# Gathering edge rows straight from `dst` and `src`: the padded copies go, and GpSimd masks the rows that were shifted back

## The chip, the cores and the metric

The kernel runs on one core of one Trainium2 chip. Its engines are named as in the profile: PE (TensorE), PEld (the weight loads of TensorE), DVE (VectorE), ACT (ScalarE), POOL (GpSimd) and SP (SyncE, which here only starts DMAs). The metric is the device time of one execution in microseconds. The kernel before took 1608.21 us, the median of three runs (1603.38 to 1609.29).

## The reference, cut to what matters

A graph has 6250 nodes with 64 features and 200,000 edges, and the edges are sorted by `dst`. Two GraphSAGE layers, then three message-passing layers with batch norm, each sum something over the edges into each node:

```python
def sage_conv(x, src, dst, W_l, b_l, W_r, n_nodes):
    msg = x[src]
    agg = jax.ops.segment_sum(msg, dst, num_segments=n_nodes)
    ...
    return mean @ W_l.T + b_l + x @ W_r.T

def _mp_layer(x, src_f, dst_f, ea_f, W, b):
    m = jnp.concatenate([x[dst_f], x[src_f], ea_f], axis=1) @ W.T + b
    agg = jax.ops.segment_sum(m, dst_f, num_segments=n)
    return jax.nn.relu(agg)
```

All five layers use the same edges. The kernel therefore builds the matrix of edge counts once (which node sends how many edges to which), and each layer is then a matrix product with it.

## The kernel before, in words

**Stages.** The first third of the execution is the build: it turns the two integer lists into 13 column tiles of the count matrix, 512 destination nodes wide, in 8-bit floats. As tiles become ready, the first SAGE layer is applied to them (`first_layer`, L724), and each tile is stored to DRAM (`adj8`, L1029). After the build come the second SAGE layer together with the edge attributes (up to 900 us or so) and the three message layers, which read the tiles back. The change touches only the build.

**Slots and columns.** The work of the build is cut into 2569 slots. A slot is a run of 128 consecutive edges together with a window of at most 10 destination nodes; 128 slots make a column t, and there are 21 columns, t = 0 to 20. `SEARCH` names five groups of columns. For each group the kernel looks up where each slot's first edge lies: `near_samples` (L824) compares samples of `dst`, `gather_behind` (L840) fetches 400 numbers behind the sample for each slot by an indirect DMA on GpSimd's queue (L843), and `first_edges` (L847) counts in them (L852) and writes the positions into `start_i` (L860, L864).

**Rows, keys, one-hots.** `fetch(t)` (L891) brings in the 128 `dst` and the 128 `src` numbers of each of the column's slots, one row of 128 numbers per partition, by two indirect DMAs on GpSimd's queue (L896) whose offsets are read from `start_i`. `columns(t)` (L900) makes two keys of them on DVE: L905 (`hi`), L906 (key 0, from the rows and `hi`), L907 (key 1), and L908, which subtracts the window's first key and clips to 2000, so that edges outside the window match nothing. PE transposes both keys (L913), ACT copies them to 16 bits, each number twice (`k2`, L915). From `k2` DVE makes one-hots (`one_hots`, L628): `lo` tiles of 16 slots, one-hot in the source, and `rhs` tiles of up to 2048 columns, one-hot in the destination. PE multiplies them slot by slot into PSUM (`pair`, L1012) and ACT moves full windows into the tile `a` (L1019, L1024).

**Padded copies.** A slot that begins fewer than 128 edges before the end of the list would read past it. So both lists are first copied into DRAM tensors `ends` (L543) that are longer by PADE (L519 to L521). Two buffers are filled on GpSimd, with 8191 for `dst` and 0 for `src` (L792, L793), and stored behind the copies (L797); 8191 is a node that no window holds. The copies themselves are two DMAs from DRAM to DRAM (L802). Column 0 does not wait for them: it reads the inputs (L894), with its starts clipped to E - 128 (L859), and the edges that the shift brings in front of the slot's own are masked by the tensor `passed` (L861, L862, L910). All later columns read `ends`.

**What sets the order.** Each engine works through its own list in order. `on_slot` (L919) fixes where the work of the next columns is called for: at slot 0 of column t `fetch(t+1)` and, at the columns that `SEARCH` names, `first_edges` or `near_samples` and `gather_behind`; at slot 64 `columns(t+1)`. `pin` keeps an instruction in the order of the program against other pinned ones; the rest a scheduler may move. Buffers set how far one engine runs ahead of another: `rows` and `key` have two (`ework`, L764), `lo` and `rhs` three each (`hot`, L765), `hi` one.

In the compiled order of before, GpSimd's list for the columns is only indirect DMAs: `fetch(t+2)` is free to go as soon as column t's keys no longer need the `rows` buffer. The transposes L913 of column t stand in PE's list at slot 96 for t = 1, 171 for t = 2, 320, 456, 577, 715, 848, 968 and so on, between none and 85 slots ahead of column t's first slot.

Of the kernel before, what the change touches and what calls it, by code (L numbers as in the profile page):

```python
# [13 lines left out]
BF16 = mybir.dt.bfloat16  # L14
F8 = mybir.dt.float8e3
I32 = mybir.dt.int32
AF = mybir.ActivationFunctionType
ALU = mybir.AluOpType
# [4 lines left out]
P = 128  # L23
# [385 lines left out]

NONE = 8191
NSMP = 4


# [2 lines left out]
EAG = 32  # L418
# [56 lines left out]
def gnn_kernel(ctx: ExitStack, tc: tile.TileContext, x, src, dst, ea, W_l1, b_l1, W_r1, W_l2, b_l2, W_r2,  # L475
# [26 lines left out]
    wins = window_plan(N, E)  # L502
# [7 lines left out]
    R = -(-NS // P)  # L510
    subs = []
    for b in range(NB):
        n, c = slots_for(expected(N, E, b * P, (b + 1) * P)), 0
# [2 lines left out]
            c += EAG  # L516
    assert len(subs) <= P
    last_b = {b: i for i, (b, _, _) in enumerate(subs)}
    PADE = P * (max(max(k for _, _, k in ws) for ws in wins) + 1)  # L519
    PADE = max(PADE, P * EAG)  # L520
    PADE = -(-PADE // 64) * 64  # L521


    c_np = np.zeros((P, 3, R + 1), np.float32)
# [15 lines left out]
    t_dram = nc.inline_tensor(t_np, name="first_edges")  # L540

    dram = ctx.enter_context(tc.tile_pool(name="fdram", bufs=1, space=DRAM))
    ends = [dram.tile([E + PADE, 1], I32, name=f"ends{i}") for i in range(2)]  # L543
    adj8 = [dram.tile([P, NB * tw(j)], mybir.dt.uint8, name=f"adj8_{j}") for j in range(NT)]
    ok_t = None

    with ExitStack() as fast:
# [203 lines left out]
        with ExitStack() as bld:  # L751
            ep = bld.enter_context(tc.tile_pool(name="edge", bufs=1))
            tab = ep.tile([P, 3, R + 1], F32, name="tab")
            etab = ep.tile([P, 3, NSUB], F32, name="etab")
            start_i = ep.tile([P, R + 1], I32, name="start_i")
# [3 lines left out]
            iota = ep.tile([P, 512], F16, name="iota")  # L759
# [4 lines left out]
            ew = slots.enter_context(tc.tile_pool(name="ework", bufs=2))  # L764
# [19 lines left out]
            thr = room[:EP, 4 * NPAD - 2 * P * (R + 1):].bitcast(mybir.dt.int16)  # L784
            early = SEARCH[1][1] * P
            t_ap = t_dram.ap() if hasattr(t_dram, "ap") else t_dram
            pad = spare(2 * PADE // 64).bitcast(I32).rearrange("p (i c) -> p i c", i=2)

            nc.sync.dma_start(smp, dst.rearrange("(p q c) -> p q c", p=EP, q=NSMP)[:, :, 0])
            nc.scalar.dma_start(thr[:, :early], t_ap[:, :early].to_broadcast([EP, early]))  # L790
            nc.scalar.dma_start(tab, c_dram.ap() if hasattr(c_dram, "ap") else c_dram)
            nc.gpsimd.memset(pad[:, 0, :], NONE)  # L792
            nc.gpsimd.memset(pad[:, 1, :], 0)  # L793
            one = pp.tile([P, 1], BF16, name="one")
            nc.gpsimd.memset(one, 1.0)
            for end, i in zip(ends, range(2)):
                pin(nc.scalar.dma_start(end[E:, :].rearrange("(p c) o -> p (c o)", p=64), pad[:64, i, :]))  # L797
            low = parts[1].rearrange("p b c -> p (b c)").bitcast(F32)
            early_weights = load_weights(low)
            for end, of, eng in ((ends[0], dst, nc.sync), (ends[1], src, nc.scalar)):  # L800

                pin(eng.dma_start(end[0: E, :].rearrange("(c p k) o -> p c (k o)", p=16, k=500),  # L802
                                  of.rearrange("(c p k) -> p c k", p=16, k=500)))
            nc.gpsimd.memset(parts[0][:, :, 3 * D: 3 * D + 1], 1.0)
            smf = pp.tile([EP, NSMP], F32, name="smf")
            nc.vector.tensor_copy(smf, smp)
# [40 lines left out]
            def first_edges(g):  # L847

                t0, t1 = SEARCH[g][0], min(SEARCH[g][1], R + 1)
                s = slice(t0, t1)  # L850
                for t in range(t0, t1):
                    pin(nc.vector.tensor_scalar(junk, blks[t % most], tab[:, 0, t: t + 1], None,  # L852
                                                ALU.is_lt, ALU.add, accum_out=c2[:, t: t + 1]))
                nc.vector.scalar_tensor_tensor(near[:, s], near[:, s], float(GAP), c2[:, s], ALU.mult, ALU.add)
                nc.vector.tensor_add(near[:, s], near[:, s], tab[:, 1, s])
                if g == 0:


                    nc.vector.tensor_single_scalar(near[:, R: R + 1], near[:, s], float(E - P), ALU.min)  # L859
                    nc.vector.tensor_copy(start_i[:, s], near[:, R: R + 1])  # L860
                    nc.vector.tensor_sub(near[:, s], near[:, s], near[:, R: R + 1])  # L861
                    nc.vector.tensor_scalar(passed, iota[:, :P], near[:, s], 4000.0, ALU.is_lt, ALU.mult)  # L862
                else:
                    pin(nc.vector.tensor_copy(start_i[:, s], near[:, s]))  # L864

            def first_attributes():

# [23 lines left out]
            def fetch(t):  # L891

                fetched[t] = rows = ew.tile([P, 2, P], I32, name="rows")
                of = [v.rearrange("(e o) -> e o", o=1) for v in (dst, src)] if t == 0 else [end[:, :] for end in ends]  # L894
                for end, i in zip(of, range(2)):
                    pin(nc.gpsimd.indirect_dma_start(  # L896
                        out=rows[:, i, :], out_offset=None, in_=end,
                        in_offset=bass.IndirectOffsetOnAxis(ap=start_i[:, t: t + 1], axis=0)))

            def columns(t):  # L900
# [4 lines left out]
                pin(nc.vector.tensor_single_scalar(hi, rows[:, 1, :], 7, ALU.logical_shift_right))  # L905
                nc.vector.scalar_tensor_tensor(key[:, 0, :], rows[:, 0, :], float(NB), hi, ALU.mult, ALU.add)  # L906
                nc.vector.scalar_tensor_tensor(key[:, 1, :], hi, -float(P), rows[:, 1, :], ALU.mult, ALU.add)  # L907
                nc.vector.tensor_scalar(key[:, 0, :], key[:, 0, :], tab[:, 2, t: t + 1], 2000.0, ALU.subtract, ALU.min)  # L908
                if t == 0:
                    nc.vector.tensor_add(key[:, 0, :], key[:, 0, :], passed)  # L910
                kp = psm.tile([P, 2, P], F32, name="lin")
# [380 lines left out]
```

## Time and profile before

| | before |
|---|---|
| median of three runs | 1608.21 us |
| the profiled execution, whole | 1605.75 us |
| its span, first to last instruction | 1604.0 us |
| granted TensorE clock | 0.977 |
| PE busy, share of the span | 1488.1 us, 93% |
| DVE busy | 905.4 us, 56% |
| ACT busy | 575.4 us, 36% |
| POOL busy, instructions | 217.7 us, 93 instructions |
| the copies to `ends` | 2 DMAs of 781.2 KB |
| `fetch` from `ends` | 40 indirect DMAs, median 3.5 us from issue to landing |
| `gather_behind` | 22 indirect DMAs, median 3.6 us from issue to landing |

The whole time is 1.75 us longer than the span. Busy shares are means over stages with different limits. Over the build (to about 540 us) DVE is busy nearly without a break for the first 200 us; over the rest of the execution PE is. In answers of the trace a row of the timeline is: start and duration in us, engine, line, operation, output and input tile, sizes, count, and in brackets the idle time before it and what ended it.

### The profile page before, as it was taken

Reading aid. Unit: us, or ns where it says so; the run is one execution under the profiler, and the core shown is the slowest. Engines: PE = TensorE matmul, PEld = TensorE weight load, DVE = VectorE, ACT = ScalarE, POOL = GpSimd, SP = SyncE. Lnnn points to the kernel's source line nnn. Section 1 sums busy time; section 2 is a strip of 40 time slices with the busy share of each in tenths; the row PEclk is TensorE's granted clock in tenths of the full one; section 3 lists DMA queues with packets and bytes.
Section 4 is the critical chain, followed back from the end, with each engine's and each line's share of the span. In section 5 each row is a group of like instructions: output and inputs, shape, how many; then the busy total and the mean of one; then the engine's idle time right before and its main releaser. Section 6 shows DMA issues by size and latency. Waiting matters only on the chain.

```text
span 1604.0 us, 38502 instructions
## 1 busy us (share of the span) xinstructions
PE 1488.1 (93%) x17115; PEld 1370.7 (85%) x17115; DVE 905.4 (56%) x1499; ACT 575.4 (36%) x1086; POOL 217.7 (14%) x93
## 2 busy tenths in 40 slices
PE   3887799999998999999999999999899999999997
PEld 2666688888886898899899989889799999899997
DVE  5899998988968509987986511111431112442222
ACT  2737476777848404544553200000310000310000
POOL 2465830731601100000000000000000000000000
PEclk9898999999999999999999999999899999899998
DMA  5302232320421536435344354443345444164540
GB/s 135 125 29 96 46 100 88 154 99 4 169 85 71 226 160 243 174 131 200 135 146 148 135 241 161 162 171 122 132 167 220 177 175 168 81 247 173 197 163 11
DMA packets 45200, 227.32 MB, mean 142 GB/s; under 512 B 23621, under 2 KB 31650, under 8 KB 37343
## 3 DMA queue, kind: packets, MB, share of 16 engines
q1 hardware_dynamic: 37965, 139.40, 23.1%
q10 hardware_dynamic: 4306, 78.10, 12.4%
q0 software_dynamic: 2752, 7.26, 1.6%
q8 instruction: 136, 2.23, 0.5%
q14 instruction: 41, 0.34, 0.1%
HBM read 183.77 MB, written 42.57 MB: 141 GB/s over the span
## 4 chain that ended last, share of the span: by engine, by line
PE 65%; DVE 17%; issue 7%; ACT 6%; DMA 3%; POOL 2%; ACTq 0%; DVEq 0%; POOLq 0%
PE agg L666 49%; PE pair L1012 7%; DVE lo L628 6%; ACT a L1019 3%; DVE rhs L628 2%; PE u L1166 2%; POOL parts L843 2%; DVE e L1070 2%; PE bank L1079 1%; DVE z L693 1%; DMA e<-in_edge_attr_dram 1%; DVE e L1072 1%; PE lin L1188 1%; PE tr L718 1%; PE lin L740 1%
## 5 line engine op out<-in xcount | busy, mean ns | idle before, releaser
L666 PE MATMUL agg<-parts,a 128*128 128x192 bf16 (+1 forms) x12005 | 1088.2, 247 | 4.4 <-DVE parts L649 1.3
L666 PEld LDWEIGHTS <-a 128*128 128x128 fp8e3 x12005 | 1006.4, 98 | 30.5 <-issue 19.6
L1019 ACT ACTIVATE a<-pair 128x784 fp8e3<-128x784 f32 (+3 forms) x355 | 294.2, 900 | 106.2 <-PE pair L1012 90.4
L1012 PE MATMUL pair<-rhs,lo 128*128 128x147 bf16 (+5 forms) x2569 | 259.4, 237 | 43.7 <-ACT a L1019 17.0
L1012 PEld LDWEIGHTS <-lo 128*128 128x128 bf16 x2569 | 191.6, 100 | 97.6 <-issue 49.2
L628 DVE TENSOR_TENSOR rhs<-iota,k 128x1960 bf16<-128x1960 f16 (+15 forms) x240 | 239.5, 1020 | 18.5 <-ACT k L915 10.5
L628 DVE TENSOR_TENSOR lo<-iota,k 128x2048 bf16<-128x2048 f16 x161 | 195.7, 1220 | 1.9 <-ACT k L915 1.3
L693 DVE TENSOR_REDUCE z<-agg 128x256 f32<-128x768 f32 (+1 forms) x39 | 35.3, 910 | 271.8 <-PE agg L666 271.4
L896 POOL DMA_INDIRECT rows<-ends,start_i x40 | 140.4, 3510 | 180.3 <-DVE key L908 154.1
L628 DVE TENSOR_TENSOR lo<-iota,e_d 128x2048 bf16<-128x2048 f16 (+11 forms) x132 | 130.9, 1012 | 19.6 <-PE bank L1079 17.6
L1079 PE MATMUL bank<-lo,lhs 128*128 128x128 bf16 x1701 | 107.6, 219 | 17.6 <-ACT lhs L1073 12.4
L1079 PEld LDWEIGHTS <-lhs 128*128 128x128 bf16 x1701 | 98.3, 98 | 29.1 <-ACT lhs L1073 20.4
L693 DVE TENSOR_REDUCE nd<-agg 128x256 f32<-128x768 f32 (+1 forms) x26 | 23.5, 907 | 116.5 <-PE agg L666 110.8
L1182 POOL TENSOR_TENSOR nd<-res,inv 128x256 f32<-128x256 f32 (+1 forms) x13 | 7.6, 588 | 550.2 <-DVE z L1128 341.2
L720 ACT COPY mx<-tr 128x512 f32<-128x512 f32 (+1 forms) x26 | 14.7, 566 | 169.7 <-PE tr L718 169.6
L709 ACT ACTIVATE sp_r<-z 128x256 f32<-128x256 f32 (+1 forms) x26 | 10.5, 403 | 172.2 <-DVE z L708 172.0
L1206 ACT ACTIVATE hr<-hr 64x512 f32<-64x512 f32 (+1 forms) x13 | 7.9, 605 | 172.2 <-DVE hr L1205 172.2
L843 POOL DMA_INDIRECT parts<-in_dst_dram,pos x22 | 53.9, 2448 | 41.0 <-DVE pos L838 31.6
L1069 ACT CAST lhs<-e 128x512 bf16<-128x512 f32 (+21 forms) x72 | 36.1, 503 | 64.0 <-PE bank L1079 43.4
L1070 DVE TENSOR_TENSOR e<-e,lhs 128x512 f32<-128x512 f32 (+21 forms) x72 | 39.5, 552 | 14.9 <-ACT lhs L1069 14.7
L1191 DVE TENSOR_SCALAR ext<-lin 64x512 f32<-64x512 f32 (+1 forms) x13 | 8.6, 663 | 68.5 <-ACT hr L1189 68.5
L1073 ACT CAST lhs<-e 128x512 bf16<-128x512 f32 (+21 forms) x72 | 36.4, 505 | 23.1 <-DVE e L1072 22.6
(149 smaller groups left out, 816.4 us busy)
## 6 DMA issues: line engine op xcount, KB each, us to landing
a<-adj SPq DMA_DIRECT2D x24, 3136.0 KB
a<-adj ACTq DMA_DIRECT2D x24, 3136.0 KB
adj<-a SPq DMA_DIRECT2D x12, 3136.0 KB
e<-in_edge_attr_dram SPq DMA_DIRECT2D x25, 256.0 KB
a<-adj SPq DMA_DIRECT2D x4, 784.0 KB
out_dram<-z SPq DMA_DIRECT2D x12, 128.0 KB
e<-in_edge_attr_dram SPq DMA_DIRECT2D x7, 152.0 KB
adj<-a SPq DMA_DIRECT2D x1, 784.0 KB
```

Of the source, the lines that this page charges most:

```text
L628: nc.vector.tensor_tensor(to.rearrange("p g (h two) -> p g h two", two=2), iota[:, :n].rearrange("p (h two) -> p h two", two=2).unsqueeze( ...
L666: nc.tensor.matmul(sums[k][:, i, :n], views[k][:, b, i * P: (i + 1) * P], pt[:, b, :n], start=(b == sources[0] and terms is None and not ( ...
L693: nc.vector.tensor_reduce(to, ps[:, :nb, : 3 * D].rearrange("p b (r d) -> p b d r", r=3), AX.X, ALU.add)
L843: pin(nc.gpsimd.indirect_dma_start(out=blks[t % most], out_offset=None, in_=dst.rearrange("(e o) -> e o", o=1), in_offset=bass.IndirectOff ...
L896: pin(nc.gpsimd.indirect_dma_start(out=rows[:, i, :], out_offset=None, in_=end, in_offset=bass.IndirectOffsetOnAxis(ap=start_i[:, t: t + 1 ...
L1012: nc.tensor.matmul(pair[:, bank % 2, col: col + wc], lo_hot(t, c), rhs[:, i, :wc], start=first, stop=last)
L1019: nc.scalar.activation(av[:, :, o: o + 2 * nd].rearrange("p h (two d) -> p h two d", two=2), pair[:, :, : nd * NB].rearrange("p two (d h) ...
L1069: nc.scalar.copy(lhs[:, :g, 0:EC], r)
L1070: nc.vector.tensor_sub(r, r, lhs[:, :g, 0:EC])
L1073: nc.scalar.copy(lhs[:, :g, 2 * EC:3 * EC], r)
L1079: nc.tensor.matmul(ps[:, :P], lhs[:, q, :], oh[:, q % HOT, :], start=(c == 0 and q == 0), stop=(i == last_b[b] and q == g - 1))
L1166: pin(nc.tensor.matmul(u[:, i, :], y[:, i * P: (i + 1) * P], maps[n - 1], start=True, stop=True))
```

## The change

- `ends`, its padding, the two fills on GpSimd, the two padding stores and the two copies are gone.
- `first_edges` clips every group's starts to E - 128 (into `c2`), writes `start_i` from the clipped value, and keeps in `c2` by how many edges each slot was shifted. This is one clip and one subtraction more on DVE for each of groups 1 to 4; group 0 had them.
- `fetch(t)` reads `dst` and `src` themselves for every t.
- In `columns(t)` for t above 0 three instructions run on GpSimd: `none` (1 where the place in the row is before the shift, times 8188 x 49), an addition of `none` to key 0, and the subtraction and clipping of key 0, which was L908 on DVE. For t = 0 the latter stays on DVE.

The changed kernel has 58 more instructions on GpSimd's list, 60 for the columns less two fills. In the compiled order GpSimd's list for a column is now: the addition and the clipping of column t, the two DMAs of `fetch(t+1)`, `none` of column t+1, then the addition and clipping of column t+1. The gathers of L843 stand between `none` and the addition of column 2 (six), of column 4 (five, behind the fill of L1038) and of column 6 (six). On PE the transposes of the keys stand at slot 101 for t = 1 and within 8 slots of where they were for all others. Off the build nothing differs.

```diff
-NONE = 8191
+NONE = 8188.0
...
-    ends = [dram.tile([E + PADE, 1], I32, name=f"ends{i}") for i in range(2)]
...
-            nc.gpsimd.memset(pad[:, 0, :], NONE)
-            nc.gpsimd.memset(pad[:, 1, :], 0)
...
-            for end, i in zip(ends, range(2)):
-                pin(nc.scalar.dma_start(end[E:, :].rearrange("(p c) o -> p (c o)", p=64), pad[:64, i, :]))
...
-            for end, of, eng in ((ends[0], dst, nc.sync), (ends[1], src, nc.scalar)):
-                pin(eng.dma_start(end[0: E, :].rearrange("(c p k) o -> p c (k o)", p=16, k=500),
-                                  of.rearrange("(c p k) -> p c k", p=16, k=500)))
...
+                nc.vector.tensor_single_scalar(c2[:, s], near[:, s], float(E - P), ALU.min)
+                pin(nc.vector.tensor_copy(start_i[:, s], c2[:, s]))
+                nc.vector.tensor_sub(c2[:, s], near[:, s], c2[:, s])
                 if g == 0:
-                    nc.vector.tensor_single_scalar(near[:, R: R + 1], near[:, s], float(E - P), ALU.min)
-                    nc.vector.tensor_copy(start_i[:, s], near[:, R: R + 1])
-                    nc.vector.tensor_sub(near[:, s], near[:, s], near[:, R: R + 1])
-                    nc.vector.tensor_scalar(passed, iota[:, :P], near[:, s], 4000.0, ALU.is_lt, ALU.mult)
-                else:
-                    pin(nc.vector.tensor_copy(start_i[:, s], near[:, s]))
+                    nc.vector.tensor_scalar(passed, iota[:, :P], c2[:, s], 4000.0, ALU.is_lt, ALU.mult)
...
-                of = [v.rearrange("(e o) -> e o", o=1) for v in (dst, src)] if t == 0 else [end[:, :] for end in ends]
-                for end, i in zip(of, range(2)):
+                for v, i in zip((dst, src), range(2)):
                     pin(nc.gpsimd.indirect_dma_start(
-                        out=rows[:, i, :], out_offset=None, in_=end,
+                        out=rows[:, i, :], out_offset=None, in_=v.rearrange("(e o) -> e o", o=1),
                         in_offset=bass.IndirectOffsetOnAxis(ap=start_i[:, t: t + 1], axis=0)))
...
-                nc.vector.tensor_scalar(key[:, 0, :], key[:, 0, :], tab[:, 2, t: t + 1], 2000.0, ALU.subtract, ALU.min)
+                if t:
+                    none = ew.tile([P, P], BF16, name="none", bufs=1)
+                    nc.gpsimd.tensor_scalar(none, iota[:, :P], c2[:, t: t + 1], NONE * NB, ALU.is_lt, ALU.mult)
+                    nc.gpsimd.tensor_tensor(key[:, 0, :], key[:, 0, :], none, ALU.add)
+                (nc.gpsimd if t else nc.vector).tensor_scalar(key[:, 0, :], key[:, 0, :], tab[:, 2, t: t + 1], 2000.0, ALU.subtract, ALU.min)
```

More of the change, by code (lines that the diff above doesn't have):

```diff
@@ L518, in gnn_kernel @@
     last_b = {b: i for i, (b, _, _) in enumerate(subs)}
-    PADE = P * (max(max(k for _, _, k in ws) for ws in wins) + 1)
-    PADE = max(PADE, P * EAG)
-    PADE = -(-PADE // 64) * 64
     c_np = np.zeros((P, 3, R + 1), np.float32)
@@ L786, in gnn_kernel @@
             t_ap = t_dram.ap() if hasattr(t_dram, "ap") else t_dram
-            pad = spare(2 * PADE // 64).bitcast(I32).rearrange("p (i c) -> p i c", i=2)
             nc.sync.dma_start(smp, dst.rearrange("(p q c) -> p q c", p=EP, q=NSMP)[:, :, 0])
```

## The prediction

> **What bounds the kernel now.** I read the busy time by stage first, because the change touches only the build. Columns: stretch, its length, then busy time (and count) of PE, PEld, DVE, ACT, POOL, the clock, DMA share and GB/s.
>
> ```profile
> 129.00:152.00 23.00, 16.91 (x159) 13.79 (x159) 23.00 (x32) 16.44 (x21) 10.08 (x1) 0.78 0.17 71
> 235.00:266.00 31.00, 29.83 (x321) 26.60 (x320) 25.49 (x35) 14.61 (x25) 3.78 (x2) 1.00 0.33 116
> 291.00:313.00 22.00, 21.76 (x261) 20.45 (x259) 22.00 (x23) 14.31 (x19) 21.74 (x1) 1.00 0.31 130
> 1250.00:1604.00 354.00, 338.00 (x3884) 331.42 (x3881) 93.07 (x224) 32.35 (x77) 0.00 (x0) 0.97 0.40 156
> ```
>
> Early in the build DVE is busy for all of 23 us and PE for 16.91: DVE sets the pace. From about 210 us PE does, with DVE close behind, in places both. After 540 us it is PE alone. POOL's 21.74 us in the third row are one single instruction, and that is the row that this change turns on. So second the timelines of POOL and DVE there.
>
> ```profile
> 235.25 1.88 POOL L896 DMA_INDIRECT rows<-ends,start_i  x1 [14.25 <-DVE key L908]
> ...
> 291.26 22.88 POOL L896 DMA_INDIRECT rows<-ends,start_i  x1 [20.93 <-DVE key L908]
> 314.45 1.98 POOL L896 DMA_INDIRECT rows<-ends,start_i  x1 [0.30 <-issue]
> ```
> ```profile
> 310.47 1.18 DVE L628 TENSOR_TENSOR rhs<-iota,k 128x1960 bf16<-128x1960 f16 x1
> 311.56 0.23 DVE L905 TENSOR_SCALAR hi<-rows 128x128 int32<-128x128 int32 x1
> 311.69 1.23 DVE L628 TENSOR_TENSOR lo<-iota,k 128x2048 bf16<-128x2048 f16 x1
> 312.83 0.30 DVE L906 SCALAR_TENSOR_TENSOR key<-rows,hi 128x128 f32<-128x128 int32 x1
> 313.03 0.30 DVE L907 SCALAR_TENSOR_TENSOR key<-hi,rows 128x128 f32<-128x128 int32 x1
> 313.23 0.29 DVE L908 TENSOR_SCALAR key<-key,tab 128x128 f32<-128x128 f32 x1
> 313.43 0.17 DVE L729 COPY cnt<-agg 128x4 f32<-128x4 f32 x1
> ```
>
> A gather whose shortest time is 0.94 us took 22.88 us. It ended at 314.14, and 0.94 us before that is 313.20: the start of L908. From 291.10 to there DVE ran one-hots (L628) and L905 to L907 without a break. The same subtraction puts the 9.20 us gather of 95.23 at 103.49 (L908 at 103.51), the 10.95 us one of 141.92 at 151.93 (L908 at 151.96), the 15.22 us one of 401.91 at 416.19 (L908 at 416.23), and the 7.76 us one of 104.73 at 111.55 (the copy L729 at 111.58). So while DVE works without a break on operations with two inputs in SBUF, an instruction of POOL that reads SBUF doesn't get in; it gets in when DVE has a gap or does something with one input, and L908 is such an opening once per column. Where DVE itself is held back by PE (235 us), POOL got in at the next end of a DVE instruction, 1.88 us.
>
> Third, how closely PE follows the keys, and the start of the build.
>
> ```profile
> 129.08 0.28 DVE L908 TENSOR_SCALAR key<-key,tab 128x128 f32<-128x128 f32 x1
> ...
> 129.42 0.44 PE L913 MATMUL lin<-ident,key 128*128 128x128 f32 x2
> ```
> ```profile
> 6.67 1.26 POOL L843 DMA_INDIRECT parts<-in_dst_dram,pos  x1 [3.89 <-DVE ext L830]
> ...
> 14.04 0.63 DVE L852 TENSOR_SCALAR_CACHE_REDUCE parts<-parts,tab 128x400 bf16<-128x400 int32 x1 [5.65 <-DMA parts<-in_dst_dram,pos]
> ```
>
> PE takes up the transposes 0.3 to 1.1 us after the start of L908 for t = 1 to 5, 7 to 9, 12, 16 and 20: it is there and waits, or nearly. For t = 6 it comes 2.6 us after, and only for t = 10, 11, 13 to 15 and 17 to 19 by 4 to 15 us.
>
> **The change, part by part.**
>
> *Copies and padding gone.* The first gather took 7.4 us from issue to use; the median of its kind is 3.6. The two copies (781.2 KB each, read and written) run just then. Nothing of the build can start before it, so their removal is worth 7.4 - 3.6 = 3.8 us at most, and nothing if the first gather is slow for another reason. I take 3.7. POOL's fills (0.14 us each) lay idle time away; `fetch` of later columns never waited for the copies.
>
> *DVE.* L908 goes: 20 times the 0.2 us between its start and its successor's, 4 us, of which the 2 us of the columns where DVE sets the pace count. Against it come 8 operations on at most 6 columns, 0.16 us long and 0.07 apart by L854 and L855: 0.5 us. The clip and copy put `start_i` one one-hot (1.2 us) later for t = 1; DVE's list takes the rows up one one-hot later too, so that is nothing.
>
> *The key on POOL.* No row shows an elementwise operation of POOL beside DVE's one-hots. Alone: the addition is half of L1182 (588 ns for 256 columns), 0.3 us; the clip and `none` like L552 on POOL, 0.54 us each. Beside one-hots I bound the wait from both sides. Below: no wait, 0.84 us for addition and clip against 0.28 of L908. Above: the gather's row, until DVE has an opening. The Trainium skill (SBUF — State Buffer, "Who interferes with whom") speaks against the change, but mildly: a DVE instruction with two SBUF inputs and a GpSimd instruction that reads SBUF exclude each other, and the later blocks until the other *instruction* has finished. By that rule each of three instructions waits at most one one-hot, 1.2 us, and the keys come 0.3 + 0.54 + 2 x 1.2 = 3.2 us after L907. By the row the wait lasts 16 to 22 us, over 10 to 19 instructions. The measurement decides: I take the row's wait where DVE sets the pace, and the rule's where PE does, as at 235 us. L908, the opening that freed the gathers, is itself removed from DVE.
>
> What ends the wait is then DVE's own want of work. PE stands at L913 and frees no `lo` or `rhs`; DVE fills the two or so free buffers of each (up to 4 x 1.15 = 4.6 us) and stops; POOL gets in. Behind PE's wait are queued its `pair` products and the first layer's; for them wait ACT and, for buffers and `k2`, DVE. DVE's loss per **stop**: addition, clip and two hand-overs of 0.3 us, 1.4; transposes 0.44 and a hand-over 0.1; some 8 to 16 products until a buffer is free, 1.1. Together 3.0 us. PE waits longer (4.6 + 1.4 = 6), but works off its store afterwards faster than DVE makes new.
>
> Column by column, by what stands ahead on POOL's list:
> - t = 1, 3, 5, 7, 9, 12, 16, 20: a stop each, 8 x 3.0 = 24.
> - t = 2: six gathers end at 68.2 us as before, DVE is near PE's pace there: 1.5.
> - t = 4: `none`, the fill (2.0) and five gathers (1.25 apart) stand ahead of the addition, and DVE has no opening between 93.6 and 111.6: 3.0 + 0.5 + 2.3 + 6.2 = 12.
> - t = 6: `none` and six gathers, 8 us, and a stop, 3; DVE has 3.7 us of L852 to do as they land and idled 1.9 there before: 6.
> - t = 8, 13, 17: `fetch(t)` now comes after the clip of t-1, one column later than before, and no opening lies between: DVE waits for rows, 0.94 and 1.5 of landing, 2.4 each, 7; t = 8 has a stop besides, 3.
> - the other columns: PE comes late enough, POOL gets in at the next end of an instruction: 0.
>
> Sum 53.5. About 4 of it fall on gaps that DVE had anyway (2.0 us between 54 and 57, for one). `none` is covered by the 20 us of a column; without that cover it would add 0.5 + a wait to each.
>
> Total: 53.5 - 4 - 3.7 - 2 + 0.5 = +44. From the profiled execution, 1605.75 + 44 = 1650; the median of the runs lies 2.5 above it: **1652 us**.
>
> **The rivals.**
> - *POOL takes its turn* (the rule holds everywhere). Keys 3.2 us late; PE has a column's 8 to 85 slots in hand, but DVE is blocked while POOL holds the port: 1.4 us in 11 columns, 15 us, less 5.2 of gains: +10, **1618 us**. For it: 235.25, 68.50 and 70.11 us, where POOL got in at an instruction's end. Against it: five waits of 9 to 23 us.
> - *Hidden, and faster* (the other side). Elementwise instructions get in at once in the 0.2 us hand-overs, or DVE's stops fall on its own slack; then 3.7 of the start and 4 of L908 remain: **1600 us**. It decides for this if POOL's two instructions end within 0.3 us or so of where L908 ended, or PE comes later than they do. For it: PE's lists allow 40 slots on average before DVE needs `k2`. Against: PE stands at L913 first.
> - *Starved throughout.* Each fetch, too, waits until DVE runs dry, in all 20 columns: 20 x (3.0 + 2.4) = 108, less 15 for DVE's slack after 210 us: **1690 to 1700 us**. For it: five instructions per column now need an opening, before two. Against: L693, L729 and L852 open several per column.
>
> **How the numbers follow.** Stops 0.62, turn-taking 0.18, hidden 0.10, starved 0.10. A measurement of this kernel can tell about 0.5% (8 us) from no change, that is 1600 to 1616. Faster: half of hidden, 0.05. Same: the other half and half of turn-taking, 0.14. Slower: the rest, 0.81. The stops' own range is 1625 to 1680 (stops of 2 to 5 us); to the turn-taking case below and part of the starved one above: 1604 to 1690.
>
> **What would show it.** Right: POOL's L895 and L896 of the changed kernel with means of many us, ending when DVE goes idle; PE waiting at its transposes for POOL's key, 3 to 8 us in each early column; DVE idle in the build up by 45 us, most before 210 us; the first L852 near 10.3 us; nothing changed behind the build but the shift. Wrong: POOL's instructions of 0.3 to 1.5 us, and PE's wait for keys as short as before. The total would be off if POOL's addition gets the port in the middle of a run of one-hots, or if late PE makes up more than I let it.

## The result, and the profile after

The changed kernel takes **1659.42 us** (median of 4 runs, 1657.8 to 1662.12) against 1605.8 us for the kernel before (4 runs, 1602.68 to 1609.29): 1.0339 times, with a 95% interval of 1.0314 to 1.0364. Its profiled execution took 1657.85 us, with a span of 1656.0 us and a granted clock of 0.959 (before: 1604.0 and 0.977). The end of the build can be read from POOL's filling of `lhs`, the first thing behind it: 588.53 us against 540.08. So 48.5 of the 52.0 us of span are lost in the build; the other 3.5 us come up again at the end of this account.

The first view is again the busy time by stage, now of the changed kernel, over the same work as the four rows of before: column 5, column 10, column 12, and the last 354 us. Columns as before.

```profile
137.90:168.10 30.20, 19.76 (x181) 16.79 (x180) 23.01 (x31) 17.16 (x21) 17.96 (x11) 0.66 0.21 78
262.80:294.20 31.40, 30.02 (x322) 26.67 (x321) 25.72 (x34) 14.10 (x24) 9.64 (x5) 1.00 0.29 110
319.60:347.70 28.10, 22.33 (x246) 21.40 (x244) 22.00 (x24) 13.17 (x17) 9.29 (x5) 0.88 0.29 120
1302.00:1656.00 354.00, 336.51 (x3881) 329.76 (x3878) 92.93 (x224) 32.29 (x77) 0.00 (x0) 0.98 0.41 156
```

DVE does the same 22 to 23 us of work in columns 5 and 12, but now stands for 7.2 and 6.1 us in them. Column 10, where PE sets the pace, and the last stage are as they were. Note the clock, the third figure from the end: 1.00 in column 12 before, 0.88 now. In column 5 it was 0.78 before already, and is 0.66.

What happens in column 5 is in three timelines of the changed kernel: first POOL, then DVE, then PE.

```profile
137.89 5.82 POOL L895 TENSOR_TENSOR key<-key,none 128x128 f32<-128x128 f32 x1 [17.25 <-DVE key L890]
143.81 0.72 POOL L896 TENSOR_SCALAR key<-key,tab 128x128 f32<-128x128 f32 x1
```
```profile
142.20 1.23 DVE L624 TENSOR_TENSOR lo<-iota,k 128x2048 bf16<-128x2048 f16 x1
147.57 1.16 DVE L624 TENSOR_TENSOR rhs<-iota,k 128x1924 bf16<-128x1924 f16 x1 [4.14 <-PE pair L1000]
```
```profile
137.80 0.42 PE L1000 MATMUL pair<-rhs,lo 128*128 128x147 bf16 x4 [0.28 <-ACT a L1007]
144.59 0.69 PE L901 MATMUL lin<-ident,key 128*128 128x128 f32 x2 [6.37 <-POOL key L896]
145.07 1.19 PE L1000 MATMUL pair<-rhs,lo 128*128 128x147 bf16 x8
```

POOL's addition (L895) takes 0.44 us where it is alone. Here it began at 137.89, the moment the keys were there, and ended at 143.71. Take 0.44 off and it really got going at 143.27; DVE's last one-hot ended at 143.43. Within 0.2 us, it was let in when DVE ran dry. PE stood 6.37 us for the key, and DVE then 4.14 us for PE. This is the stop of the prediction.

Over the whole build, these two groups of the changed kernel's page carry it (busy time, mean ns of one; idle time ahead and what ended it):

```profile
L895 POOL TENSOR_TENSOR key<-key,none 128x128 f32<-128x128 f32 x20 | 57.7, 2887 | 270.8 <-DVE key L890 211.6
...
L901 PE MATMUL lin<-ident,key 128*128 128x128 f32 x42 | 11.7, 367 | 60.9 <-POOL key L896 51.8
```

To see which columns stopped, I took the time from one column's `hi` to the next in both traces and subtracted. Eight columns grew by 4.5 us or more: 2 (4.6), 3 (6.7), 5 (7.2), 8 (4.5), 9 (7.6), 12 (6.1), 16 (5.1) and 20 (6.9), together 48.7 us. The other twelve grew by 3.7 us in all. The start is 3.9 us earlier. 48.7 + 3.7 - 3.9 = 48.5.

Column 2 is not like the other seven. Its addition was not shut out by one-hots; it stood on POOL's list behind six gathers (the last begins at 64.21 us) and then took the 0.44 us that it takes alone:

```profile
65.42 0.44 POOL L895 TENSOR_TENSOR key<-key,none 128x128 f32<-128x128 f32 x1
```

In three kernels below PE does not wait for POOL at all. There column 2 still grows by 4.2, 0.4 and 6.3 us, while column 1 shrinks by 3.9, 1.1 and 2.7 us. How much of its 4.6 us is POOL's is therefore not settled.

The start, in DVE's timeline of the changed kernel: the first count was at 14.04 us before.

```profile
10.16 0.63 DVE L839 TENSOR_SCALAR_CACHE_REDUCE parts<-parts,tab 128x400 bf16<-128x400 int32 x1 [1.67 <-DMA parts<-in_dst_dram,pos]
```

And one thing the prediction did not have: the clock around the stop of column 12, in the changed kernel's busy time by stretch.

```profile
320.50:323.00 2.50, 0.76 (x8) 0.38 (x5) 2.50 (x3) 0.91 (x2) 2.50 (x1) 1.00 1.13 482
323.00:326.90 3.90, 0.00 (x0) 0.00 (x0) 2.76 (x3) 0.00 (x0) 3.76 (x2) 0.78 0.96 412
326.90:328.50 1.60, 1.58 (x9) 1.45 (x10) 0.00 (x0) 0.58 (x1) 1.06 (x2) 0.50 0.01 0
328.50:330.50 2.00, 2.00 (x15) 1.83 (x14) 0.09 (x1) 0.83 (x1) 1.66 (x2) 0.50 0.25 66
330.50:333.00 2.50, 2.50 (x23) 2.40 (x21) 1.09 (x1) 0.83 (x1) 0.00 (x0) 0.70 0.00 0
```

PE is idle for 5.59 us (to 326.92). When it restarts, the granted clock is 0.50, and it stays below 1.00 for about 5 us, just when DVE waits for the products.

### The profile page after: what moved, and what is told of

It reads as the page before. It is cut to its first block, busy times and chain, and to the rows that moved or that the text cites. A ratio compares the mean times of both kernels' runs of the same rounds, so it can differ in the third digit from the quotient of the medians.

```text
span 1656.0 us, 38564 instructions
## 1 busy us (share of the span) xinstructions
PE 1500.3 (91%) x17115; PEld 1387.3 (84%) x17115; DVE 906.9 (55%) x1487; ACT 575.9 (35%) x1086; POOL 208.5 (13%) x151
## 4 chain that ended last, share of the span: by engine, by line
PE 48%; DVE 10%; DMA 3%; ACT 2%; issue 2%; POOL 0%; SPq 0%; ACTq 0%; DVEq 0%; POOLq 0%
PE agg L662 41%; DVE lo L624 4%; DMA e<-in_edge_attr_dram 2%; PE u L1154 2%; DMA a<-adj 2%; PE bank L1067 1%; DVE e L1058 1%; DVE z L689 1%; DVE e L1060 1%; PE lin L1176 1%; PE lin L1175 1%; PE pair L1000 1%; PE agg L669 0%; PE tr L714 0%; ACT lhs L1061 0%
## 5 line engine op out<-in xcount | busy, mean ns | idle before, releaser
L1000 PE MATMUL pair<-rhs,lo 128*128 128x147 bf16 (+5 forms) x2569 | 269.0, 244 | 34.1 <-ACT a L1007 15.2
L1000 PEld LDWEIGHTS <-lo 128*128 128x128 bf16 x2569 | 203.2, 104 | 81.2 <-issue 42.7
L1067 PE MATMUL bank<-lo,lhs 128*128 128x128 bf16 x1701 | 107.5, 219 | 17.9 <-ACT lhs L1061 12.1
L895 POOL TENSOR_TENSOR key<-key,none 128x128 f32<-128x128 f32 x20 | 57.7, 2887 | 270.8 <-DVE key L890 211.6
L901 PE MATMUL lin<-ident,key 128*128 128x128 f32 x42 | 11.7, 367 | 60.9 <-POOL key L896 51.8
L901 PEld LDWEIGHTS lin<-ident,key 128*128 128x128 f32 x42 | 5.7, 174 | 64.2 <-POOL key L896 55.1
L1057 ACT CAST lhs<-e 128x512 bf16<-128x512 f32 (+21 forms) x72 | 36.1, 502 | 63.3 <-PE bank L1067 40.4
```

The costliest lines, as they stand in the source:

```text
L895: nc.gpsimd.tensor_tensor(key[:, 0, :], key[:, 0, :], none, ALU.add)
L901: nc.tensor.transpose(kp[:, i, :], key[:, i, :], ident)
L1000: nc.tensor.matmul(pair[:, bank % 2, col: col + wc], lo_hot(t, c), rhs[:, i, :wc], start=first, stop=last)
L1057: nc.scalar.copy(lhs[:, :g, 0:EC], r)
L1067: nc.tensor.matmul(ps[:, :P], lhs[:, q, :], oh[:, q % HOT, :], start=(c == 0 and q == 0), stop=(i == last_b[b] and q == g - 1))
```

## The experiments

The theory: an instruction of POOL that reads SBUF is shut out while DVE runs one-hots without a break; PE waits for its result and DVE for PE. Rivals: POOL and DVE take turns and the loss is something else; POOL, once it is in, slows DVE itself; TensorE's order has the transposes too early.

The kernel before ran beside each group of kernels again, and its median was 1605.8, 1612.9, 1615.7, 1615.9 and 1605.3 us. So beside each ratio I give the build's end in the profile (before 540.1, changed 588.5). Unless an edit says so, nothing of the reference's computation is left out.

### POOL's part undone: mask and clip on DVE

```diff
-                    nc.gpsimd.tensor_scalar(none, ...)
-                    nc.gpsimd.tensor_tensor(key[:, 0, :], key[:, 0, :], none, ALU.add)
-                (nc.gpsimd if t else nc.vector).tensor_scalar(key[:, 0, :], ...)
+                    nc.vector.tensor_scalar(none, ...)
+                    nc.vector.tensor_tensor(key[:, 0, :], key[:, 0, :], none, ALU.add)
+                nc.vector.tensor_scalar(key[:, 0, :], ...)
```

> The changed kernel with the mask, its addition and the clip on DVE for all columns; copies gone, rows gathered from the inputs as in the changed kernel. Theory (POOL's key instructions are shut out by DVE's two-input one-hots until DVE runs dry): no stops; DVE pays two more instructions per column, 0.2 us each in about 11 columns where it sets the pace (+4 us), and the start stays 3.8 us earlier: 1606 us, 1601 to 1612. Rival 1 (the loss comes from gathering from the inputs, or from fetch standing one column later): it stays at 1650 us or more. Rival 2 (the loss is the extra work of the mask, wherever it runs): 1620 us or more.

Measured: 0.9957 of before (0.9943 to 0.997), build's end 537.2. The longest wait of PE for a key is 0.15 us. Two more instructions per column on DVE than before (the clip was there) cost 0.5 to 0.7 us in columns 3, 4, 5 and 7; the other columns move both ways, by up to 4.2 us. The removed copies give 4.0 us at the start. So the whole loss hangs on POOL's part, and without it the change gains slightly.

### POOL's part alone: only the clip of before on POOL

```diff
-                nc.vector.tensor_scalar(key[:, 0, :], ..., ALU.subtract, ALU.min)
+                (nc.gpsimd if t else nc.vector).tensor_scalar(key[:, 0, :], ..., ALU.subtract, ALU.min)
```

> The kernel before, padded copies and all, with one instruction alone moved: the subtraction and clip of the key from DVE to POOL for columns above 0. Theory: one instruction of POOL in the way of the transposes is enough for a stop, shorter by the addition (0.5 us): 9 stops of 5 to 6 us, 1606 + 45 to 50 = 1652 us, and POOL's clip takes up to 5 to 6 us where it runs alone in 0.7. Rival 1 (copies or gathers): 1606 us. Rival 2 (cost goes by the number of POOL's instructions, three before, one here): about 1606 + 18 = 1624 us.

Measured: 1.0228 (1.0197 to 1.0259) of a before of 1612.9; build's end 584.1, that is 44.0 us later. The clip, 0.72 us alone, takes 3.40 us on average, and the same eight columns stop. From this kernel's page:

```profile
L908 POOL TENSOR_SCALAR key<-key,tab 128x128 f32<-128x128 f32 x20 | 68.0, 3398 | 298.7 <-DVE key L906 235.2
```

One instruction makes 44.0 of the 52.4 us (48.5 + 3.9) that three make: the price hangs on PE waiting for POOL at all, hardly on how much POOL does.

### POOL works, but nobody waits

POOL's instructions run as in the changed kernel, but their results go to a tile that is not read; the clip, and for the last column the mask, are on DVE.

```diff
-                    nc.gpsimd.tensor_tensor(key[:, 0, :], key[:, 0, :], none, ALU.add)
+                    nc.gpsimd.tensor_tensor(none, key[:, 1, :], none, ALU.add)
+                    nc.gpsimd.tensor_scalar(none, none, tab[:, 2, t: t + 1], 2000.0, ALU.subtract, ALU.min)
...
```

> The changed kernel's three POOL instructions per column, in the same places of POOL's list, reading the same keys but writing to a tile that nobody reads; the clip is back on DVE, with the mask (on DVE) only in the last column. Theory: POOL is shut out as long or longer (instructions of 5 to 20 us), but PE doesn't wait for it: 1602 us, 1597 to 1609, and no waits of PE for POOL. Rival 3 (POOL's instructions cost because they hold the port and block DVE, 1.9 us per column): 1602 + 20 = 1622 us or more. Rival 1 (gathers): 1650 us.

Measured: 1.0106 (1.0073 to 1.014), a miss. All columns grow by 1.6 us at most, except 12 (11.1) and 16 (10.8). There POOL's timeline, and then DVE's, show why:

```profile
288.05 20.80 POOL L895 TENSOR_TENSOR none<-key,none 128x128 bf16<-128x128 f32 x1 [14.36 <-DVE key L891]
308.95 0.72 POOL L896 TENSOR_SCALAR none<-none,tab 128x128 bf16<-128x128 bf16 x1
309.94 1.05 POOL L880 DMA_INDIRECT rows<-in_dst_dram,start_i  x1 [0.27 <-issue]
311.29 0.94 POOL L880 DMA_INDIRECT rows<-in_src_dram,start_i  x1 [0.30 <-issue]
```
```profile
319.60 0.23 DVE L889 TENSOR_SCALAR hi<-rows 128x128 int32<-128x128 int32 x1 [11.04 <-DMA rows<-in_src_dram,start_i]
```

With nobody waiting, nothing makes DVE run dry, and the addition is shut out for 20.80 us. Queued behind it are the gathers of column 13, and DVE then idles 11.04 us for its rows. The rival that POOL slows DVE itself is out as the cause of the loss: POOL runs the same three instructions in every column, and no other column grows by more than 1.6 us. But "harmless if nobody waits" was wrong too: someone waits for what is queued behind.

### An opening made by hand

The changed kernel, with a useless one-input reduction (12 x 128 numbers) on DVE one instruction behind the keys.

```diff
+                if t:
+                    opened = ew.tile([P, 12], F32, name="opened", bufs=1)
+                    pin(nc.vector.tensor_reduce(opened, key[:, 1, :].unsqueeze(1).to_broadcast([P, 12, P]), AX.X, ALU.add))
```

> The changed kernel with one useless reduction on DVE (one input of 12 x 128, about 1.65 us[...]) close behind the keys of each column above 0, so that POOL finds the port free. Theory: POOL's addition and clip then take about 0.5 and 0.7 us, ending in or just after the reduction; PE's waits for POOL fall from 52 us to under 15; DVE pays 1.65 us in the 11 or so columns where it sets the pace, 18 us, for stops of 5 to 7 us in 9: 1659 - 52 + 18 = about 1625 us, 1612 to 1640. Rival 4 (POOL is simply late by its own slowness and its queue): the reduction is added on top, 1677 us. Rival 1: 1677 us too.

Measured: 1.0127 (1.0096 to 1.0158), build's end 562.0. POOL's additions in this kernel (minimum, median and maximum in ns):

```profile
L895 POOL TENSOR_TENSOR key<-key,none x20: 424/1402/1467, 43.7 to 540.1; 128x128 f32<-128x128 f32 x20
```

None is above 1.47 us, where the changed kernel has 5.85. DVE was given about 30 us more to do (busy 936.7 against 906.9 us), and the kernel is 26.5 us earlier at the build's end. It is the kind of DVE's instructions, not how busy DVE is, that shuts POOL out for long.

### The keys taken up later

TensorE's transposes moved from some 50 slots ahead of their use to 8.

```diff
-                    nc.tensor.transpose(kp[:, i, :], key[:, i, :], ident)
+                    pin(nc.tensor.transpose(kp[:, i, :], key[:, i, :], ident))
...
+                if c == 120 and t + 1 < R:
+                    turn(t + 1)
```

> The changed kernel with the transposes of a column's keys put 8 edges ahead of their use (edge 120 of the column before, instead of some 50 ahead) in TensorE's order. Theory (POOL gets in only when VectorE runs dry or at an opening): time alone does not help; TensorE goes on for longer, so VectorE goes on for longer too and the addition stays shut out; in the columns without an opening between edge 64 and 120 the stop comes at edge 120 instead, with no work of the next column prepared, so it costs as much or more: 1645 to 1670, and additions of 10 us and over appear on POOL. Rival (TensorE's order merely has the transposes too early, and POOL gets in by itself in the meantime): nearly all comes back, 1603 to 1612.

Measured: 1.0074 (1.0047 to 1.01), build's end 556.8: neither theory's number. As the theory says, the additions get longer, to 11.67 us. But two thirds of the loss is gone. In columns 3, 5 and 8 an opening came by in the meantime (a one-input DVE operation at 85.47, 136.47 and 193.74 us). Where none came, as in column 12 (POOL, then DVE, of this kernel), DVE ran out of keys:

```profile
297.41 10.26 POOL L895 TENSOR_TENSOR key<-key,none 128x128 f32<-128x128 f32 x1 [16.24 <-DVE key L890]
```
```profile
309.68 1.18 DVE L624 TENSOR_TENSOR rhs<-iota,k 128x1960 bf16<-128x1960 f16 x1 [2.30 <-ACT k L912]
```

That stop costs 3.4 us instead of 6.1, and PE waited only 0.78 us for the key. Its key transposes take 0.27 us at the median, in the changed kernel 0.42. I had priced a stop at the end of the column as high as one in the middle.

### Fewer buffers

```diff
-            hot = slots.enter_context(tc.tile_pool(name="hot", bufs=3))
+            hot = slots.enter_context(tc.tile_pool(name="hot", bufs=2))
```

> The changed kernel with two buffers instead of three for VectorE's one-hots. Theory (POOL's addition is let in when VectorE's lead is used up): the lead is one buffer of up to 8 one-hots shorter, so the longest additions fall from 5.8 us to some 3 to 4, and TensorE's waits for the keys from up to 6.4 us to some 3 to 4; the total gains at most a few us, because the lead that is not built up is not there to be lived on either: 1650 to 1665. Rival (the addition's 5.8 us are a fixed price of sharing with VectorE): the additions and the waits stay as they are.

Measured: 1668.04 us in one run. In columns 3, 5 and 8 the additions fall from 5.7, 5.8 and 4.7 us to 3.5, 3.6 and 2.5, as expected: there, how long POOL is shut out is how long DVE has free buffers. In column 11 the addition took longer, 6.05 instead of 1.45 us. The total is slightly worse than expected: column 4 grows by 8.2 us, with PE waiting 9.03 us for its key, and column 11 by 10.6. I put this down to the lead that DVE no longer has; no run shows it apart.

### What a stop costs: the clock and the place

The stop was put at 3.0 us and measures 6.1. Three edits of TensorE's order look for the rest. The first puts 14 useless transposes of the identity ahead of the key transposes in the eight stopping columns, so that PE works while it waits.

```diff
+                if t in (2, 3, 5, 8, 9, 12, 16, 20):
+                    for _ in range(14):
+                        pin(nc.tensor.transpose(kp[:, 0, :], ident, ident))
```

> The changed kernel with 14 useless transposes (of the identity, into the tile that the key transposes then overwrite) ahead of the key transposes in the eight columns that stop (2, 3, 5, 8, 9, 12, 16, 20): 14 x 0.27 = 3.8 us of TensorE work inside waits of 3.4 to 6.4 us, so TensorE idles under 2.6 us at a time. Theory (each stop costs 6.1 us and not 3.0 because TensorE restarts at a granted clock of 0.50): the clock stays at 1.00 behind the stops, the key transposes take 273 ns instead of 417, and the first products free VectorE's buffer some 1.4 us earlier: 8 x (0.3 + 1.4) = 13.6 us less than the changed kernel, about 1644 to 1650, 1.024 to 1.028 of before. Rival (VectorE and POOL alone set the stop's length, the clock falls on time that is lost anyway): as the changed kernel, 1.033. If the clock stays at 0.50 behind the stops although TensorE was busy, the run says nothing on this.

Measured: 1.0149 (1.0126 to 1.0173), build's end 571.5. In column 12 of this kernel PE idles 3.37 us, and its key transposes take 0.44 us and not 0.69. The gain is larger than expected (1.024 to 1.028). But the edit had also moved the key transposes 1 to 17 slots forward in six columns, so it does not tell the clock from the place. The next one keeps the places (577, 969, 1089, 1476, 2001, 2499; only column 2 stands at 192 instead of 171).

> The same 14 useless transposes ahead of the key transposes of the eight stopping columns, but with these at the places in TensorE's order that the changed kernel has (edges runs 577, 969, 1089, 1476, 2001, 2499 and so on). The run before with 14 transposes had them 1 to 17 runs earlier as well, on or next to multiples of 16, where a 16-slot tile of one-hots has just been used up and nothing more is missing to free it; so its gain (1.0149 of before instead of 1.0339) mixes the clock and the place. Theory (the clock is most of it): key transposes of 273 ns and products at full rate behind the stops, 1.015 to 1.022 of before. Rival (the place is most of it: VectorE still waits for some 20 products until a tile comes free): 1.026 to 1.033. In between, both, shared as the number says. What stands in column 5 decides too: in the changed kernel 2.98 us from the transposes to VectorE's next one-hot over 20 products; full rate would make it about 2.

Measured: 1.0228 (1.0212 to 1.0243) of a before of 1615.9, build's end 585.0. The number lies between the two ranges, and column 5's 2.99 us did not shrink. But it decides nothing on the clock: the 14 transposes took 1.69 us, PE still idled 3.0 to 5.0 us, and in six of the eight columns the key transposes still took 0.69 us. So a third with more of them, side by side with the changed kernel and the first once more.

> The transposes stay at the changed kernel's places; the useless ones ahead of them are now 14, 26, 38, 24, 32, 34, 26 and 26 in columns 2, 3, 5, 8, 9, 12, 16 and 20. The run before had 14 everywhere and they took only 1.69 us (0.12 each, not 0.27), so TensorE still idled 3.4 to 5.0 us and restarted at 0.50 in six of the eight columns: it did not test the clock. At 0.12 us each these fill the waits but for 1.5 to 2.5 us. Theory (restart at half clock is a good part of each stop): granted clock near 1.00 behind the stops of columns 8 to 20, key transposes 0.44 us instead of 0.69, 0.25 + about 1 us less VectorE idle per stop, build end some 8 to 12 us earlier than the changed kernel's 588.5, that is 576 to 581. Rival (place alone made the difference): build end 584 to 589, as in the run before (585.0).

> The changed kernel itself, unchanged, as the yardstick for the two runs beside it: the kernel before took 1612.9 to 1615.9 us in the later calls and 1605.8 in the first, so ratios of different calls cannot be subtracted to a few tenths of a per cent. Every theory expects a span near 1656 us in the profile; the ratio is 1.034 if the chip scales both kernels alike, and about 1.027 if only what lies behind the build scatters (52 us less the 10 that before has gained in the median).

> The kernel with 14 useless transposes and the places 1 to 17 runs earlier, once more, so that it stands beside the changed kernel in one call: build end 571.5 as before and 14 to 18 us below the changed kernel in the median. The difference to the run with warm TensorE in place is what the place is worth: about 5 to 10 us if the clock's part is 8 to 12, and 13 to 17 if the clock does nothing.

Measured side by side:

| | of before (1605.3) | build's end |
|---|---|---|
| changed kernel | 1.0321 (1.0293 to 1.0348) | 587.2 |
| PE warm, same place | 1.0269 (1.0249 to 1.0288) | 584.0 |
| 14 transposes, earlier place | 1.0217 (1.0198 to 1.0236) | 576.8 |

Column 16 shows the clock at work. First PE's timeline of the changed kernel in this group and its busy time over the 5.8 us from the restart, then both for the kernel with PE warm:

```profile
440.94 0.69 PE L901 MATMUL lin<-ident,key 128*128 128x128 f32 x2 [4.64 <-POOL key L896]
441.43 1.02 PE L1000 MATMUL pair<-rhs,lo 128*128 128x98 bf16 x10
```
```profile
440.94:446.74 5.80, 5.79 (x53) 5.56 (x54) 2.43 (x3) 3.40 (x4) 2.73 (x3) 0.50 0.42 164
```
```profile
438.08 0.44 PE L914 MATMUL lin<-ident,key 128*128 128x128 f32 x2 [2.29 <-POOL key L896]
438.36 1.40 PE L1020 MATMUL pair<-rhs,lo 128*128 128x98 bf16 x20
```
```profile
438.08:443.88 5.80, 5.76 (x71) 5.49 (x72) 3.88 (x4) 4.44 (x6) 3.69 (x3) 0.71 0.43 170
```

Ten products in 1.02 us against twenty in 1.40, a mean clock of 0.50 against 0.71 (with PE warm it falls to 0.50 too, but only about 0.8 us after the restart); DVE stands 2.54 us there instead of 4.06. In columns 5, 8 and 16, where the key transposes took 0.44 us, the column grows by 4.9, 2.5 and 3.1 us instead of 6.6, 4.5 and 5.1. POOL's additions there are as long as in the changed kernel (5.82, 4.72 and 4.10 us), so the gain is not theirs. In 9, 12 and 20 the key transposes took 0.63 to 0.69 us all the same.

The eight stops together lose 15.4 us less (32.2 instead of 47.6). Not all of this is the clock: 6.2 us are column 3, where POOL's addition took 1.45 us and not 5.71. Here the changed kernel, then the one with PE warm:

```profile
85.12 5.71 POOL L895 TENSOR_TENSOR key<-key,none 128x128 f32<-128x128 f32 x1 [14.02 <-DVE key L890]
```
```profile
85.48 1.45 POOL L895 TENSOR_TENSOR key<-key,none 128x128 f32<-128x128 f32 x1 [12.43 <-DVE key L890]
```

DVE ran the same one-hots behind the key both times, without a break; why POOL got in at the first hand-over in one kernel is not shown. And columns 1, 4, 10, 11, 14 and 17, which the edit was not to touch, lose 12.1 us more, 4.7 of them in column 4. In 10, 11 and 17 the scheduler had moved the key transposes by 4 slots; for 1, 4 and 14 the reason is not shown. So the build's end gains 3.2 us where I expected 8 to 12. At 584.0 it lies in the range that I had given the rival: the total speaks for the place, and only the columns speak for the clock.

The kernel with the earlier place ends its build another 7.3 us sooner: column 9 grows by 3.4 us instead of 7.3. This is not the place alone, since the two kernels have different numbers of useless transposes, and 3.7 of the 7.3 us are column 4. In column 5 DVE's next one-hot starts 2.99 us after the key transposes in the changed kernel, 2.45 with PE warm at the same place (slot 577), and 0.54 with the transposes one slot earlier. POOL's addition is shorter there too, 3.61 us instead of 5.82, because DVE runs dry two one-hots sooner:

```profile
134.78 3.61 POOL L895 TENSOR_TENSOR key<-key,none 128x128 f32<-128x128 f32 x1 [17.25 <-DVE key L890]
```

Fewer products then lie between the transposes and the next buffer that comes free (5 instead of 14); which buffer it is I did not take apart.

### The mask where it is needed only

In these inputs only the last column's rows begin within 128 edges of the end. Clip on DVE, mask on DVE for that column alone.

```diff
-                if t:
+                if t == R - 1:
```

> The start of the changed kernel with the clip back on VectorE and the mask (none and addition) on VectorE for the last column alone, the only one whose rows can begin within 128 edges of the lists' end. Theory: what made the changed kernel slower is POOL's part alone, and removing the copies is worth the start's 3.8 us. Then it stands below the version with the mask on VectorE in every column (0.9957 of before): that one paid about 0.3 us of VectorE in each of some 14 columns where VectorE sets the pace, 4 us. Expected 0.992 to 0.995 of before (about 1595 of 1605.8). Rival: the 0.5 us per column there came from something else than the two added instructions (the transfers' new order, say), then it stays at 0.9957 or above.

Measured: 0.9959 (0.9941 to 0.9977), build's end 539.4: not better than the mask everywhere, a miss. The start is 4.3 us earlier, but column 2 grows by 6.3 us: DVE stands 6.0 us there, and PE, in the same column, 4.57 us for ACT's `parts` (L634). I did not follow this further. Both versions take 0.4% less than the kernel before.

## Why the prediction was right, and where it was not

Predicted were 1652 us, within 1625 to 1680; measured are 1659.42. The mechanism, stops of DVE because PE waits for POOL, is the one that the runs show. That the number came so near is in part luck, as the sum by columns shows.

**What bounds the kernel.** Right: the growth lies in eight columns, and in six of them (2, 3, 5, 8, 12, 16) DVE had no idle time before. DVE's idle time in them is up by about 48 us (45 predicted), but only some 23 of it lies in columns 2, 3, 5 and 8; "most before 210 us" was too much.

**Copies.** 3.7 us were put down for the start; it is 3.9. The kernel that keeps the copies and moves only the clip starts 0.6 us earlier than before, those without the copies about 4: the copies, with their padding, were what made the start slow.

**Row against rule.** Right to take the row. The Trainium skill ("SBUF — State Buffer", "Who interferes with whom") has the later instruction wait for the other's end. In column 5 POOL stayed shut out through five DVE instructions, and for 20.80 us when nobody stopped DVE. Elsewhere the rule held: in columns 1, 10, 11, 17 and 19 POOL got in at the first hand-over, although DVE made no pause. Column 10 of the changed kernel, POOL and then DVE:

```profile
263.35 1.45 POOL L895 TENSOR_TENSOR key<-key,none 128x128 f32<-128x128 f32 x1 [22.65 <-DVE key L890]
```
```profile
264.43 1.39 DVE L624 TENSOR_TENSOR rhs<-iota,k 128x1924 bf16<-128x1924 f16 x1
```

The one-hot behind the hand-over took 1.39 us where one of its size takes 1.16 (column 5 above). I drew the line between row and rule at whether PE or DVE paces; column 1, priced as a stop, and column 3 with PE warm lie on the wrong side of it, so what decides is open. "Turn-taking" and "hidden" fell as accounts of the whole, and so did "starved throughout": once DVE is dry, the fetches behind the clip take 1.05 and 0.94 us.

**The step that failed: "Together 3.0 us".** A stop costs 6.1 us on average, 48.7 / 8. From DVE's last one-hot to the transposes it is 1.16 us in seven of the eight (I had 1.5: the addition 0.44 and the clip 0.72 instead of 0.3 and 0.54, without the hand-overs that I had added). From there to DVE's next one-hot it is 2.9 us on average where I had 1.54: transposes 0.69 and not 0.44, and products at a clock of 0.50. Together 4.2 us (33.6 / 8). The other 1.9 us come after it. I wrote that PE "works off its store afterwards faster than DVE makes new"; after these stops it did not, and DVE stands again: 3.04 us in column 5 at 156.21, for PE's L822, and 1.45 us in column 12. With PE warm the wait for L822 is 0.95 us.

Of the 3.1 us missing per stop, the restart at half clock accounts for 1.7 to 2.0 in the three columns where it was put off in place (5, 8 and 16). The place of the transposes against the 16-slot tiles is a second part: column 9 grows by 3.4 us with the earlier place, where the changed kernel grows by 7.6. Their shares in the total are not settled, since the edits that kept PE warm moved other columns as well.

The Trainium skill ("TensorE: Matmul & The Clock Gate", Part 1) states what I should have weighed here: after a window of about 3.4 us without work TensorE's clock is halved, and as long a busy one brings it back. By that rule a wait that I had put at 6 us had to cost the clock as well, and the eight stops agree: 0.50 at the restart, after waits of 3.51 to 6.37 us. As a threshold the rule does not fit the traces: the kernel before has 10 us at half clock in the same column 5, though PE had not waited longer than 1.45 us in the 12 us ahead of them:

```profile
141.50:151.60 10.10, 8.98 (x62) 7.89 (x63) 10.10 (x14) 5.41 (x7) 9.68 (x1) 0.50 0.37 159
```

So the stops added half-clock time to what was there: the mean clock from 20 us to the build's end is 0.96 before and 0.91 in the changed kernel, which makes an estimated 42 and 102 us at half clock (twice what the mean lacks of 1.00, times the stretch).

**Column by column.** The sum was 53.5 and came to 52.4 (48.7 + 3.7), by errors that cancel. Against the stops at 6.1 instead of 3.0, and column 2 (1.5 predicted, 4.6 measured), stand: column 4 (12 predicted, 0.5 measured) and column 6 (6, and -0.2), where the five and six gathers ahead of the addition were through as PE came, and its remaining waits of 3.65 and 2.92 us cost DVE next to nothing; columns 1 and 7 (a stop each; 0.9 and 0.5, their additions took 1.47 and 0.48 us); and the late fetch for columns 8, 13 and 17 (7; nothing in 13 and 17 beyond 1.1). That last mechanism is real: it is the whole loss of the run in which nobody waits. In the changed kernel each stop clears POOL's list.

**DVE.** The 2 us gained by the missing L908 and the 0.5 for small operations do not show by themselves; they are within the 3.7 us of the quiet columns.

**Behind the build.** "Nothing changed but the shift" holds. The first profile of the changed kernel has 3.5 us more behind the build than before, 2.7 of them because PE waits 3.74 us for a tile of `a` at 622.75, where before it waited 1.08. But the second profile of the same kernel waits 1.03 us there, and has 1063.9 us behind the build, as the kernel before has. These 3.5 us differ between executions and are not the change's.

## What to carry to other kernels

Before an operation is handed to GpSimd, look at what VectorE does at that moment: if it runs two-input SBUF operations without a break, GpSimd's instruction may not end until VectorE runs dry, however short it is, and everything queued behind it is late too. If TensorE waits for the result, add a restart at half clock to the price of the wait. Here twenty clips of 0.28 us kept on VectorE were worth 44 us.

## What the runs showed of the hardware that was not expected

- Behind the waits of 3.51 to 6.37 us of the eight stops the key transposes took 0.69 us instead of 0.44, and the granted clock was 0.50 for 4 us and more in the two taken apart (in column 5 of the changed kernel up to 154 us, 9.4 us after the restart; in column 12 for about 5 us). No sharp threshold shows. After 3.65 us ahead of column 4 the key transposes took 0.44 us in the changed kernel and 0.69 in the one with the earlier place; after 3.07 us ahead of column 16, 0.44 us in one run and 0.69 in another of the same kernel; and after 2.67 us in column 12 of the kernel with PE warm, 0.69.
- How long POOL is shut out has no bound seen here: 20.80 us for an addition of 0.44 us. A single one-input operation of DVE lets it in (L895 at most 1.47 us). A hand-over between two one-hots sometimes does and sometimes does not: in column 3, behind the same one-hots of DVE, the addition took 5.71 us in one kernel and 1.45 in another.
